# First loads over other queues, identity products ahead of the first tile, and later quarters of the output weights in a two-layer attention kernel

## The chip, the core and the metric

The kernel runs on one core of a Trainium2 chip, in float32 throughout. The metric is the device time of one execution in microseconds (us). A core has a matrix engine (TensorE, PE in the profile, with PEld for its weight loads), VectorE (DVE), ScalarE (ACT), GpSimd (POOL) and SyncE (SP), which only issues transfers. Each works through its own instructions in order. SyncE, ScalarE and GpSimd issue the DMAs, which 16 DMA engines carry out.

## What is computed

The input has 8 images of 32x32 tokens with 512 channels. Layer 0 is a group norm, queries, keys and values by one weight matrix, softmax attention with 8 heads, an output product and a residual. Layer 1 is an attention whose keys and values are sampled at learned positions, then a product with a gelu and a residual.

```
x_norm = group_norm(x, 32 groups) * scale + bias
q, k, v = split(x_norm @ w_qkv + b_qkv)
x = x + softmax(q k^T / 64) v @ w_out + b_out                # layer 0
q = layernorm(x) @ wq + bq;  where = tanh(pw(gelu(depthwise7x7(q))))
kv = bilinear(x, where) @ wv + bv
z = x + softmax((q@mq_w + mq_b) (kv@mk_w + mk_b)^T) (kv@mv_w + mv_b) @ mo_w + mo_b
out = z + gelu(layernorm(z) @ mlp_w + mlp_b)                 # layer 1
```

## The kernel before

**Order of the work.** Layer 0 runs in units: a unit is 128 queries of one pair of heads, so an image has 32 (`per`), and the 8 images have 256. `push` (L206) of a unit emits its scores, then the steps that `run_due` (L371) finds due before the unit's place plus 0.8, then the transposes of the exponentials, every second unit the transfers of both, and then the steps due before the end of the unit. Other work is put into this order by `at(place, step)`, where a place is a number of units. Steps with negative places run ahead of the first unit, sorted by place. The class `InOrder` (L43) fixes each engine's instructions in the order of the program, so all of them carry one line number, L54, in the profile, and one tells them apart by their tiles.

**The start.** Image 0's eight x tiles (128 tokens by 512 channels, 256 KB each) are loaded first (L525 to L530): tiles 0 to 3 by GpSimd's queue, 4 to 7 by SyncE's. SyncE's queue then has three small vectors (gsc, gbi, bqkv, one 4-byte element at a time onto the partitions), then the three 1 MB parts of w_qkv in the order keys (`wB`), queries (`wA`), values (`wC`), and three 256 KB rows (L532 to L537, L550 and L551). `norm_steps` (L569) makes the norm of an image: `turn(t)` transposes tile t by four TensorE products with an identity, and ScalarE copies it out of PSUM into `xT`; `two_tiles` takes statistics of each pair of tiles by four VectorE instructions; `gather`, `means`, `deviations` and `factors` form the group's mean and deviation, with two small TensorE products; `norm` applies them to xT. For image 0 the places are -100 plus `norm_places`, so tiles 0 and 1 are at -91.6 and -91.55, tiles 2 and 3 at -83.6 and -83.55, tiles 4 to 7 at -77.6, -77.55, -76.6 and -76.55. Only then come the keys' products with wB. `turn(0)` and `turn(1)` of image 0 also load the next image's tiles 0 and 1 by GpSimd's queue. PSUM has three buffers for such products, used in turn. `warm(3)`, at two places of the start, gives TensorE three products with an identity (each in two halves, 512 columns) that nobody reads.

**Attention transfers.** The transposed exponentials of two units go through 16 SyncE transfers of 128 KB (`moved`, L222: `et<-sq`), and the products `av<-et,v` of these units follow some three units later (`attention_out`, L767).

**The last image.** Layer 1's weights are folded together while the last image's attention runs (`fold_steps`, L800). The buffer `room_w["w"]`, tag `w`, holds one 1 MB weight matrix at a time; the last image's has wv until its transposes at 23.5 to 24.55 units after the image's begin, then w_out, by quarters of 256 KB that ScalarE's queue issues (`load_quarter`, L545) at 25.2, 25.7, 26.2 and 26.7. Quarters of mv_w follow at 27.2, 27.9, 28.6 and 29.3 by the same queue. The products of the fold that stand among them are at 25.5, 27.5, 28.5, 29.5, 30.5 and 31.5; w_out is first read at 33.1 (`last_places`, L787).

Of the kernel before, what the change touches and what calls it, by code (L numbers as in the profile page):

```python
# [17 lines left out]
P = 128  # L18
# [3 lines left out]
C = 512  # L22
# [4 lines left out]
NQT = QB // P  # L27
NH = 8
HD = 64
# [219 lines left out]
def attention_then_deformable_attention(  # L249
# [30 lines left out]
    nc = tc.nc  # L280
    x_tok = x.rearrange("b h w c -> b (h w) c")
# [8 lines left out]
    ident = const.tile([P, P], F32, tag="ident", name="ident")  # L290
# [7 lines left out]
    def mm_tile():  # L298
        return ps_mm.tile([P, QB], F32, tag="mm", name="mm")

    def by_chunk(w):
        return w.rearrange("(c p) o -> p c o", p=P)
# [65 lines left out]
    def at(place, step):  # L368
        due.append((place, len(due), step))
# [40 lines left out]
    def kept(name):  # L410
        return keep.tile([P, NC, C], F32, tag=name, name=name)
# [98 lines left out]
    with ExitStack() as l0:  # L510
# [3 lines left out]
        nc = InOrder(tc)  # L514
        NX = 2
        NX_T = 3
        xs = {}

        def load_x(b, t):
            if b < B:  # L520
                xs[b, t] = work.tile([P, C], F32, tag="x", name="x", bufs=NX)
                nc.gpsimd.dma_start(xs[b, t], x_tok[b][ts(t, P), :])
# [2 lines left out]
        x2 = work.tile([P, NC, QB], F32, tag="xT", name="x2", bufs=NX_T)  # L525
        for t in range(NQT):
            xs[0, t] = work.tile([P, C], F32, tag="attT", name="x0", bufs=NQB * NHP)
            nc.gpsimd.dma_start(xs[0, t], x_tok[0][ts(t, P), :])
            xs[0, NQT + t] = x2[:, t, :]
            nc.sync.dma_start(xs[0, NQT + t], x_tok[0][ts(NQT + t, P), :])  # L530
        w3 = [kept(name) for name in ("wA", "wB", "wC")]
        gsc = load_cols(wp, gn_scale, "gsc")  # L532
        gbi = load_cols(wp, gn_bias, "gbi")
        bqkv = load_cols(wp, b_qkv, "bqkv")
        for i in (1, 0, 2):
            nc.sync.dma_start(w3[i], by_chunk(w_qkv)[:, :, ts(i, C)])
        bout = load_row(wp, b_out, "bout")  # L537
        room_w = {}

        def load_weight(w):  # L540

            room_w["w"] = work.tile([P, NC, C], F32, tag="w", name="w", bufs=1)
            nc.gpsimd.dma_start(room_w["w"], by_chunk(w))

        def load_quarter(w, c):  # L545
            if c == 0:
                room_w["w"] = work.tile([P, NC, C], F32, tag="w", name="w", bufs=1)
            nc.scalar.dma_start(room_w["w"][:, c, :], by_chunk(w)[:, c, :])
# [10 lines left out]
            out=g3, in_=g3, pattern=[[-GRP, ng], [0, GRP]], compare_op=ALU.is_ge,  # L559
# [3 lines left out]
            out=g3, in_=g3, pattern=[[GRP, ng], [0, GRP]], compare_op=ALU.is_ge,  # L563
# [5 lines left out]
        def norm_steps(b, start, places):  # L569

            room = {}

            def turn(t):
                blk, i = divmod(t, NQT)
                if i == 0:
                    xTs[b, blk] = work.tile([P, NC, QB], F32, tag="xT", name="xT", bufs=NX_T)
                if t == 0:
                    room["stats"] = work.tile([P, NC, NT // 2, 6], F32, tag="stats", name="stats", bufs=1)
                ps = mm_tile()
                for c in range(NC):  # L580
                    nc.tensor.transpose(ps[:, ts(c, P)], xs[b, t][:, ts(c, P)], ident)
                nc.scalar.copy(xTs[b, blk][:, :, ts(i, P)], ps.rearrange("p (c q) -> p c q", q=P))
                if b > 0:
                    load_x(b + (t + NX) // NT, (t + NX) % NT)
                elif t < NX:
                    load_x(1, t)

            def two_tiles(i):
                blk, half = divmod(i, NQT // 2)
                for c in range(NC):  # L590
                    nc.vector.bn_stats(
                        room["stats"][:, c, i, :], xTs[b, blk][:, c, ts(half, 2 * P)]
                    )


            def gather():
                mv = room["mv"] = work.tile([P, NC, 2], F32, tag="mv", name="mv")
                stats = room["stats"]
                for c in range(NC):
                    nc.vector.bn_aggr(mv[:, c, :], stats[:, c, :, :].rearrange("p s f -> p (s f)"))  # L600

            def means():
                mv = room["mv"]
                ps = mm_tile()
                for m in range(2):
                    half = ds(m * HD, HD)
                    nc.tensor.matmul(
                        ps[half, 0:NC], lhsT=gmat[:, half], rhs=mv[:, :, 0], start=True, stop=True
                    )
                mu = room["mu"] = work.tile([P, NC], F32, tag="mu", name="mu")  # L610
                nc.vector.tensor_copy(mu, ps[:, 0:NC])
                dev = room["dev"] = work.tile([P, NC], F32, tag="dev", name="dev")
                nc.vector.tensor_tensor(dev, mv[:, :, 0], mu, ALU.subtract)
                nc.vector.tensor_tensor(dev, dev, dev, ALU.mult)
                nc.vector.tensor_tensor(dev, dev, mv[:, :, 1], ALU.add)

            def deviations():
                ps = mm_tile()
                for m in range(2):
                    half = ds(m * HD, HD)  # L620
                    nc.tensor.matmul(
                        ps[half, 0:NC], lhsT=gmat[:, half], rhs=room["dev"], start=True, stop=True
                    )
                room["rs"] = work.tile([P, NC], F32, tag="rs", name="rs")
                rstd(room["rs"], ps[:, 0:NC], 1e-6)

            def factors():
                nc.vector.tensor_tensor(room["rs"], room["rs"], gsc, ALU.mult)
                room["add"] = work.tile([P, NC], F32, tag="nadd", name="nadd")
                nc.vector.tensor_tensor(room["add"], room["mu"], room["rs"], ALU.mult)  # L630
                nc.vector.tensor_tensor(room["add"], gbi, room["add"], ALU.subtract)

            def norm(blk):
                xT, add, rs = xTs[b, blk], room["add"], room["rs"]
                for c in range(NC):
                    if b == 0 and c % 2 == 0:
                        nc.vector.tensor_scalar(
                            xT[:, c, :], xT[:, c, :], rs[:, c : c + 1], add[:, c : c + 1],
                            ALU.mult, ALU.add,
                        )  # L640
                    else:
                        nc.scalar.activation(
                            xT[:, c, :], xT[:, c, :], AF.Identity,
                            bias=add[:, c : c + 1], scale=rs[:, c : c + 1],
                        )

            steps = [
                *(lambda t=t: turn(t) for t in range(NT)),
                *(lambda i=i: two_tiles(i) for i in range(NT // 2)),
                gather, means, deviations, factors,  # L650
                *(lambda blk=blk: norm(blk) for blk in range(NQB)),
            ]
            for place, what in zip(places, steps):
                at(start + place, what)
# [145 lines left out]
        def fold_steps(first):  # L800
# [41 lines left out]
                nc.scalar.dma_start(raws[name][:, c, :], by_chunk(w)[:, c, :])  # L842

            for c in range(NC):
                at(first + 25.2 + 0.5 * c, lambda c=c: load_quarter(w_out, c))
                at(first + 27.2 + 0.7 * c, lambda c=c: quarter("mv", mv_w, c))
                at(first + per + 1.24 + 0.001 * c, lambda c=c: quarter("wq", wq, c))
            for i, place in enumerate((25.5, 27.5, 28.5, 29.5)):
# [158 lines left out]
        def warm(n):  # L1007
            out = mm_tile()
            for c in range(n):
                for m in range(2):  # L1010
                    half = ds(m * HD, HD)
                    nc.tensor.matmul(
                        out[half], lhsT=ident[:, half], rhs=xTs[0, 0][:, 0, :],
                        start=(c == 0), stop=(c == n - 1),
                    )

        norm_steps(0, -100, norm_places)
        for place in (-76.035, -74.5):
            at(place, lambda: warm(3))
        at(-72.5, lambda: load_weight(w_out))  # L1020
        at(-73, lambda: nc.vector.tensor_scalar(bqkv[:, 0:NC], bqkv[:, 0:NC], 1.0 / HD, None, ALU.mult))

# [13 lines left out]
        for b in range(B):  # L1036
            first = b * per
# [22 lines left out]
            for hp in range(NHP):  # L1060
                for qt in range(NT):
                    n = first + hp * NT + qt
                    if n % per == 0 and b > 0:
# [9 lines left out]
                    t = qkv[b, hp]  # L1073
# [4 lines left out]
                        at=qt % NQT,  # L1078
# [8 lines left out]
    with ExitStack() as l1:  # L1087
        nc = tc.nc


        def pool(name, bufs=1):
            return l1.enter_context(tc.tile_pool(name=name, bufs=bufs, reuse_waits="tile"))

        late, late2, cv, cvhat, first, raw, wp = (
            pool(n) for n in ("late", "late2", "cv", "cvhat", "first", "raw", "w2")
        )
        work = pool("work1", 2)
        nc = InOrder(tc)
# [447 lines left out]
```

## Time and profile before

| what | us |
|---|---|
| median of three runs | 3269.66 |
| lowest, highest | 3261.96, 3269.79 |
| the profiled execution, its own time | 3264.03 |
| its span, from the first to the last instruction | 3262.3 |
| TensorE busy in it | 3217.9 (99%) |
| DVE, ACT, POOL busy | 2522.9, 1780.8, 1593.5 |
| first TensorE product | begins at 8.37 |
| first product of keys | begins at 23.04 |
| longest wait of TensorE after the first 24 us | 2.69, before 2061.11 |

How to read it: the profile is of one execution, with times from its first instruction. "out<-in" are tiles by the program's names, "xN" a number of instructions. "SPq" and "ACTq" are issues of transfers, with the time that the issue held the queue's engine. In the list of waits, "A <- B: total, times, longest" says that A was released by B. PEclk is the granted TensorE clock, 1.00 being full. The trace also records when each of a transfer's 16 parts completed; a transfer has landed with the last.

### The profile page before, as it was taken

How to read it: one execution, taken by the hardware profiler on the slowest of the kernel's cores; microseconds unless marked ns; L12 is line 12 of the kernel's file. 1: busy time of each engine (PE TensorE's matmuls, PEld its weight loads, DVE VectorE, ACT ScalarE, POOL GpSimd, SP SyncE). 2: the span in 40 equal slices, each digit the busy share in tenths (PEclk: the TensorE clock that was granted, in tenths of full speed). 3: DMA queues.
4: the chain of work that ended last, by engine and by line, in shares of the span. 5: the costliest groups of instructions: out<-in, count | busy, mean ns of one | idle time of the engine just before them, and what ended most of it. 6: DMA issues, size and time to landing. Idle time of an engine off the chain costs nothing.

```text
span 3262.3 us, 59564 instructions
## 1 busy us (share of the span) xinstructions
PE 3217.9 (99%) x21588; PEld 1301.2 (40%) x21588; DVE 2522.9 (77%) x3457; ACT 1780.8 (55%) x3826; POOL 1593.5 (49%) x2026
## 2 busy tenths in 40 slices
PE   8999999999999999999999999999999999999999
PEld 4444344344344444444444434333333333333333
DVE  5776778898888888788788888557868787676765
ACT  3443356566567567557657656335555555554442
POOL 1001316755764665664674577225556565653323
PEclk9999999999999999999999999999999999999999
DMA  5666766777677766676676677678777786887873
GB/s 171 169 179 162 210 181 180 211 200 186 204 196 191 203 197 177 204 211 178 181 223 183 177 216 211 180 228 272 219 240 242 228 264 211 264 259 229 265 236 130
DMA packets 479325, 674.31 MB, mean 207 GB/s; under 512 B 76828, under 2 KB 268632, under 8 KB 478776
## 3 DMA queue, kind: packets, MB, share of 16 engines
q1 hardware_dynamic: 434528, 529.53, 56.8%
q0 software_dynamic: 41136, 136.78, 13.7%
q10 hardware_dynamic: 3368, 4.20, 0.4%
q8 instruction: 171, 2.80, 0.4%
q14 instruction: 122, 1.00, 0.1%
HBM read 263.17 MB, written 138.69 MB: 123 GB/s over the span
## 4 chain that ended last, share of the span: by engine, by line
PE 89%; DVE 3%; ACT 2%; DMA 2%; POOL 1%; issue 1%; SPq 1%; POOLq 0%; DVEq 0%; ACTq 0%
PE mm L54 55%; PE sc L54 17%; PE av L54 17%; ACT e L54 1%; DVE nmax L54 1%; SPq L54 1%; DMA et<-sq_d 1%; DVE sq L54 1%; POOL oa L54 0%; DVE chunk L54 0%; DMA w<-in_L_conv_w_out_dram 0%; DMA sq_d<-sq 0%; POOL xr L54 0%; DMA row<-mid,ii 0%; ACT part_x L54 0%
## 5 line engine op out<-in xcount | busy, mean ns | idle before, releaser
L54 ACT ACTIVATE e<-sc,nmax 128x1024 f32<-128x1024 f32 (+1 forms) x1024 | 803.0, 797 | 531.4 <-DVE nmax L54 524.7
L54 DVE TENSOR_REDUCE nmax<-sc 128x1 f32<-128x1024 f32 (+1 forms) x640 | 750.2, 1212 | 291.3 <-PE sc L54 286.0
L54 POOL TENSOR_TENSOR oa<-part_x,oa 128x256 f32<-128x256 f32 x852 | 639.4, 751 | 542.5 <-ACT part_x L54 496.4
L54 DVE STREAM_TRANSPOSE sq<-e 128x1024 f32<-128x1024 f32 x640 | 764.3, 1225 | 118.5 <-ACT e L54 97.7
L54 ACT ACTIVATE part_x<-pad_x,dww_x 128x256 f32<-128x256 f32 x852 | 441.2, 545 | 259.9 <-POOL oa L54 258.4
L54 PE MATMUL sc<-k,q 64*64 64x512 f32 x4096 | 512.3, 603 | 8.8 <-ACT e L54 6.7
L54 PE MATMUL av<-et,v 128*64 128x256 f32 x4096 | 499.2, 386 | 11.7 <-DMA et<-sq 4.5
L54 PEld LDWEIGHTS av<-et,v 128*64 128x64 f32 x4096 | 273.7, 137 | 328.8 <-issue 162.1
L54 POOL TENSOR_TENSOR mv<-mv,minus_half 128x1 f32<-128x1 f32 x128 | 76.3, 596 | 389.0 <-DVE mv L54 388.0
L54 PEld LDWEIGHTS sc<-k,q 64*64 64x64 f32 x4096 | 137.5, 132 | 314.6 <-issue 208.4
L54 POOL TENSOR_TENSOR chunk<-parts,chunk 128x256 f32<-128x256 f32 x240 | 185.3, 772 | 137.2 <-ACT parts L54 123.2
L54 DVE SCALAR_TENSOR_TENSOR od<-pad_x,dww_x,od 128x256 f32<-128x256 f32 x276 | 232.7, 843 | 5.5
L54 PE MATMUL mm<-wo,attH 128*64 128x512 f32 x1024 | 233.7, 598 | 0.0
L54 PE MATMUL mm<-wC,xT 128*64 128x256 f32 x2048 | 232.1, 379 | 0.0
L54 PE MATMUL mm<-xT,wB 128*64 128x512 f32 x1024 | 230.7, 592 | 0.6 <-DVE xT L54 0.6
L54 PE MATMUL mm<-hat_h,wA 128*64 128x512 f32 x1024 | 230.9, 593 | 0.0
L54 PE MATMUL mm<-xT,wA 128*64 128x512 f32 x1024 | 230.7, 592 | 0.0
L54 PE MATMUL mm<-w,attT 128*64 128x512 f32 x1024 | 230.1, 592 | 0.3 <-DMA w<-in_L_conv_w_out_dram 0.3
L54 PE MATMUL mm<-wm,zT 128*64 128x512 f32 x976 | 220.7, 592 | 0.5 <-ACT zT L54 0.5
L54 ACT ACTIVATION_READ_ACCUMULATOR e<-sc,nmax 128x1 f32 x1024 | 209.1, 204 | 0.0
L54 PEld LDWEIGHTS mm<-wC,xT 128*64 128x64 f32 x2048 | 148.0, 137 | 77.7 <-issue 6.4
L54 PE MATMUL mm<-w,hat_x 128*64 128x512 f32 x768 | 170.2, 593 | 0.0
(198 smaller groups left out, 3457.6 us busy)
## 6 DMA issues: line engine op xcount, KB each, us to landing
et<-sq SPq DMA_DIRECT2D x2048, 128.0 KB
sq_d<-sq SPq DMA_DIRECT2D x128, 512.0 KB
et<-sq_d SPq DMA_DIRECT2D x128, 512.0 KB
inv<-rs_d SPq DMA_DIRECT2D x250, 128.0 KB
xr<-mid POOLq DMA_DIRECT2D x64, 256.0 KB
xr<-in_x_dram POOLq DMA_DIRECT2D x62, 256.0 KB
x<-in_x_dram POOLq DMA_DIRECT2D x60, 256.0 KB
out_dram<-res POOLq DMA_DIRECT2D x60, 256.0 KB
```

The source lines that it names most:

```text
L54: return self.tc.keep_in_program_order(op(*args, **kwargs))
```

## The change

Five edits:

1. Image 0's tiles 0 to 3 go by SyncE's queue and 4 to 7 by GpSimd's, the reverse of before.
2. SyncE's queue loads only the queries' and values' weights. The keys' (`wB`) are issued by ScalarE's queue, at place -83.54, which is after ScalarE's copy of tile 3.
3. `warm_ident(5)` is emitted ahead of all steps: five products of the identity with itself, each in two halves of 64 by 128 columns, into a PSUM buffer that nobody reads.
4. The next image's tiles 0 and 1 are loaded at place -70, after the load of w_out, not in `turn(0)` and `turn(1)`.
5. The last image's quarters of w_out are at 29.7, 30.2, 30.7 and 31.2.

```diff
-            nc.gpsimd.dma_start(xs[0, t], x_tok[0][ts(t, P), :])
+            nc.sync.dma_start(xs[0, t], x_tok[0][ts(t, P), :])
             xs[0, NQT + t] = x2[:, t, :]
-            nc.sync.dma_start(xs[0, NQT + t], x_tok[0][ts(NQT + t, P), :])
+            nc.gpsimd.dma_start(xs[0, NQT + t], x_tok[0][ts(NQT + t, P), :])
...
-        for i in (1, 0, 2):
-            nc.sync.dma_start(w3[i], by_chunk(w_qkv)[:, :, ts(i, C)])
+
+        def load_qkv(i, queue):
+            queue.dma_start(w3[i], by_chunk(w_qkv)[:, :, ts(i, C)])
+
+        for i in (0, 2):
+            load_qkv(i, nc.sync)
...
                 if b > 0:
                     load_x(b + (t + NX) // NT, (t + NX) % NT)
-                elif t < NX:
-                    load_x(1, t)
...
-                at(first + 25.2 + 0.5 * c, lambda c=c: load_quarter(w_out, c))
+                at(first + 29.7 + 0.5 * c, lambda c=c: load_quarter(w_out, c))
...
+        def warm_ident(n):
+            out = mm_tile()
+            for c in range(n):
+                for m in range(2):
+                    half = ds(m * HD, HD)
+                    nc.tensor.matmul(
+                        out[half, 0:P], lhsT=ident[:, half], rhs=ident,
+                        start=(c == 0), stop=(c == n - 1),
+                    )
+
         norm_steps(0, -100, norm_places)
+        warm_ident(5)
+        at(-83.54, lambda: load_qkv(1, nc.scalar))
         for place in (-76.035, -74.5):
             at(place, lambda: warm(3))
+        for t in range(NX):
+            at(-70, lambda t=t: load_x(1, t))
         at(-72.5, lambda: load_weight(w_out))
```

## The prediction

> **What bounds the kernel now.** I read first the page's chain of work that ended last: TensorE is 89% of it, and the page has it busy 3217.9 of 3262.3 us. So an edit counts only where TensorE waits or runs slowly, and I looked for these places. Two are near the change. The first is the start, by the chain of the first 24 us (columns: start, length, what; small pieces left out):
>
> ```profile
> 1.39 6.84 DMA x<-in_x_dram
> ...
> 8.37 5.88 PE mm L54 x24
> ...
> 14.27 0.59 ACT xT L54
> ...
> 14.88 2.71 DVE stats L54 x8
> ...
> 19.49 2.93 PE mm L54 x16
> ```
>
> Nothing runs until tile 0 has landed (8.23, by GpSimd's queue); then transposes, copies and statistics follow each other to 17.52. SyncE's and ScalarE's timelines of this stretch (start, length, queue or engine, what):
>
> ```profile
> 0.79 1.81 SPq L54 DMA_DIRECT2D x<-in_x_dram  x4
> 2.65 0.43 SPq L54 DMA_DIRECT2D gsc<-in_L_conv_gn_scale_dram  x1
> ...
> 4.46 7.95 SPq L54 DMA_DIRECT2D wB<-in_L_conv_w_qkv_dram  x1
> 12.45 0.51 SPq L54 DMA_DIRECT2D wA<-in_L_conv_w_qkv_dram  x1
> ```
> ```profile
> 11.71 0.59 ACT L54 COPY xT<-mm 128x512 f32<-128x512 f32 x1 [0.52 <-PE mm L54]
> 12.56 0.59 ACT L54 COPY xT<-mm 128x512 f32<-128x512 f32 x1 [0.27 <-PE mm L54]
> 13.41 0.59 ACT L54 COPY xT<-mm 128x512 f32<-128x512 f32 x1 [0.27 <-PE mm L54]
> 14.27 1.64 ACT L54 COPY xT<-mm 128x512 f32<-128x512 f32 x3 [0.27 <-PE mm L54]
> ```
>
> The issue of wB held SyncE for 7.95 us. The copies stand 0.85 us apart up to 14.27 and closer after it: four transposes take 0.85 us with 230 ns weight loads up to 14.2, and 0.43 us with 140 ns ones from 14.4. So TensorE ran at half its later rate for 6 us, though PEclk shows 1.00 there.
>
> The second place is the last image's stretch by TensorE's timeline, SyncE's list of waits, and the table by windows (length, engines' busy time, PEclk, DMA share, GB/s):
>
> ```profile
> 2061.11 2.51 PE L54 MATMUL av<-et,v 128*64 128x256 f32 x16 [2.69 <-DVE rs L54]
> 2063.34 4.84 PE L54 MATMUL mm<-raw 128*64 128x512 f32 x16
> ```
> ```profile
> SPq L54 <- DMA raw<-in_L_conv_mv_w_dram: 5.5, 2, 4.6
> ...
> SPq L54 <- DMA w<-in_L_conv_w_out_dram: 4.8, 2, 4.4
> ```
> ```profile
> 2061.10:2066.00 4.90, 4.89 (x24) 2.74 (x26) 2.46 (x3) 1.03 (x2) 3.08 (x4) 0.65 0.74 181
> ```
>
> The wait of 2.69 is named after VectorE, but the last of the 16 transfers of et landed at 2060.92; it was that. SyncE stood from 2043.1 to 2047.55 before the third of them. SyncE's and ScalarE's transfers take eight completion counters in turn, and an issue waits until the counter's transfer before it has landed. The counter here was the second quarter of w_out's, issued by ScalarE at 2042.22 and landed at 2047.53. So 4.4 us of SyncE's wait became TensorE's 2.69, and the clock, granted at 0.65 in the last row, took more: 2.51 and 4.84 us where the same groups take 1.95 and 3.60 elsewhere, 1.8 us.
>
> **The change, part by part.**
>
> *Tiles swapped.* The landings belong to the queues: SyncE's tiles landed at 3.50, 4.11, 9.24 and 9.85 (the last two by one or two late engines of 16), GpSimd's at 8.23, 9.40, 10.51 and 11.20. Swapped, tiles 0 and 1 are transposed at about 4 to 6.5, and then TensorE waits for tile 2 until 9.24. Tile 2 began at 10.55 before, so 1.25 us are won there. From 9.3 on, six tiles at the slow 0.85 us end at 14.4; no later tile waits (11.20 is the latest landing). Tile 7's copy ends at 14.4 + 0.2 + 0.6 = 15.2 (before: 15.91), its four statistics of 0.33 at 16.6 (before: 17.52): **-0.9**. `warm(3)` (2.79) then runs at the fast rate from 14.45 to 17.25, just in time for the next product. If tiles 2 and 3 land with their first 14 engines (6.6 and 7.8) and the transposes run at the fast rate, GpSimd's last tile at 11.20 sets the end: 11.65 transposed, 12.4 copied, and VectorE's 2.7 us of the last two pairs done by about 14.6: -2.9.
>
> *Identity products.* Five, two halves each: between 5 x 0.21 and 5 x 0.43 us by the transposes' and the three-product group's rows, from about 2.6 (identity written at 2.51). They end by 4.8, a little after tile 0's landing at 3.50, and the wait for tile 2 hides that: 0. I give them no gain either, since TensorE is idle again from 6.5 to 9.3 before the bulk of the transposes. Without that wait they would cost tile 0 up to 1.3 us. The trace needed six busy us, transposes alone, before the rate rose. The Trainium skill, "TensorE: Matmul & The Clock Gate", Part 4, says that transposes do not count as activity for the clock; here the rate doubled in the midst of transposes, so I go by the row. By the page the identity products would be the only activity before `warm`, and all transposes would stay slow: that sum is also -0.9.
>
> *wB on ScalarE.* Copies 4 to 7 and the norm are queued behind this issue, and TensorE's tile 7 waits for copy 4's buffer. It costs from 0.34 (ScalarE's own quarters of w_out) to 7.95 (wB on SyncE). I take 0.5, as wA and wC took, since that queue is empty. It begins after copy 3, at 11.85; copy 4 would have begun at 12.05, so 0.3 is late there and is caught up by copy 6: 0. Should it take gsc's counter, it waits for 12.72 at most, which costs about 0.3. SyncE's long issue becomes wA's. wA and wB then move together: wB, wA and wC landed 2.7 us apart (17.34, 20.05, 22.76), so the two take 5.4 from about 13.3 and are there by 19. Keys' products can begin at 22.1, so it is covered by 3 us; without that cover each late us counts. The skill's "DMA: Bandwidth & Descriptors", section "Issuing engines are not separate DMA queues", speaks against this edit: another issuer saves issue time alone. The trace's 392 GB/s with one queue agrees, and nothing is claimed for it here.
>
> *Next image's tiles.* Two issues of 0.55 us leave GpSimd's queue at 5.2 and come back at 21.9, ahead of bq_x, dww_x and a memset of 1.4 us that are used units later; the tiles are first read some 60 us after. 0. Their 0.5 MB leave the stretch up to 12.5, which helps gsc.
>
> *Quarters of w_out later.* Counters go round in the program's planned order, not by when ScalarE really issues. Without the quarters the 16 transfers begun at 2041.84 take 16 x 0.652 and 2.7 to land, 2055 against the need at 2058.4. The stall goes, and the slow clock with it: -2.69 - 1.8 = **-4.5**. What is late next: the quarters now stand around the transfers that begin at 2075.11. In the order of before, a quarter at a place ending in .2 fell behind 10 or 11 of the sixteen two units earlier, at .7 behind 12, 16 or 6. Carried over, the last mv quarter holds the first of these transfers by 0.9 us, w_out's quarters the third by 1.1 and the seventh by 1.7: 3.7 together, against a slack of 2.3 (landed at 2087.6, used at 2090.06). A new stall of 3.7 - 2.3 = **+1.4**; from 0 (planned otherwise) to 4.5 (the whole of the old one). I take 1.4, without a slow clock, since gaps of about 1 us (1.06 at 356.9, 0.98 at 421.9) had none. w_out lands near 2086, some 10 us before it is read at 2100.43.
>
> **Sum.** -0.9 - 4.5 + 1.4 = -4.0. From the profiled execution, 3264.03 (span 3262.3 and 1.7 around it), that is 3260.0. That execution lies 5.6 under the median of the runs, 3269.66. The four shown (3261.96, 3264.03, 3269.66, 3269.79) spread over 7.8 us, and nothing tells which level the next will have, so I set the sum against their mean, 3266.4: **3262.4**.
>
> **The rivals.**
> - *The stall only moves* (chance 0.25). The later quarters meet the last sixteen transfers with the old 2.69 and the slow clock. For it: the mechanism is the same and the slack is 2.3. Against: DMA engines are busier in the old place (share 1.00 at 2047 to 2053, 0.72 at 2072 to 2078). Only -0.9 is left: 3265.5.
> - *Both parts in full* (0.2): tiles 2 and 3 not late, no new stall: -2.9 - 4.5 = -7.4, 3259.0. Against: the late engines are there in the trace.
> - *ScalarE held by wB* (0.1). The issue lasts 7.95 us there too, from 11.85 to 19.8, if what held SyncE is not SyncE's queue alone. Copies 4 to 7 then run to 22.1 and statistics to 23.4, 5.9 later than before; with -3.1 of the last image the kernel is slower by 2.8: 3269.2. Statistics end 3.6 us after copy 4 begins, so the start loses from an issue that ends after 13.9, and the whole from 17.0. Against: wA, behind wB on the same queue, took 0.51.
> - *The start does not move* (0.05): the products or the wait of the counter take what the swap gives; -3.1, 3263.3.
>
> The forecast has 0.4. **Range:** the best case from the lowest run is 3254.6, the held ScalarE from the highest 3272.6; with 2 in 10 left outside, 3256 to 3271. About 0.3% (9.8 us) is what a measurement of this kernel can tell from no change. No case alone reaches it; but with runs that spread over 7.8, a median under 3259.9 comes about in half of the full case and a sixth of the others but the held one: 0.1 + 0.12 = 0.22 faster. Slower needs 3279.5, the held case from the highest level and more: 0.03. Within 0.3%: 0.75.
>
> **What would show it.** Right: TensorE's first transposes of x near 4, a wait of some 3 us for tile 2, copy 7 done near 15.2, keys' products from about 22.1; no wait before `av` near 2057, PEclk 1.00 there, SyncE's waits for w_out's quarters 30 us later and a wait of TensorE of 1 to 2 us near 2085. Wrong: an issue of wB on ACTq of several us, tiles 2 and 3 landing elsewhere than near 9.5, the rate of the transposes doubling before tile 4, or the old wait still there.

## The result, and the profile after

The changed kernel is slower by 0.3%: median 3274.27 us (22 runs, 3267.66 to 3293.23) against 3265.27 for the kernel before (22 runs, 3257.91 to 3272.07), ratio 1.0029 with a 95% interval of [1.0020, 1.0038]. The forecast was 3262.4, which is 4.0 below the 3266.4 that it was set against; the result is 9.0 above the kernel before. The profiled execution after took 3270.45 us, its span is 3268.6; before, 3264.03 and 3262.3.

I set the two traces side by side by the begin of each unit's first exponential (ScalarE's `e<-sc`), which both have in the same order. After minus before, in us:

| at unit | difference | what lies between this row and the one above |
|---|---|---|
| 0 | -2.15 | the start |
| 58 (469 us) | -3.2 | |
| 83 (679 us) | +0.55 | a wait of 2.71 before `av` at 614.58, and a half clock from 614.5 to 617.9 |
| 242 | +1.8 | small waits |
| 253 | -2.7 | the old wait at 2061 is gone |
| 256 | +4.5 | a wait of 3.16 at 2090.23, and one of 4.08 at 2164.56 with a half clock |
| end of the span | +6.25 | |

The start, by the changed kernel's TensorE timeline (start, length, what, count, and in brackets the wait ahead of it):

```profile
2.57 2.40 PE L54 MATMUL mm<-ident 128*64 128x128 f32 x20 [2.57 <-POOL ident masks.py:199]
4.90 1.97 PE L54 MATMUL mm<-ident,x 128*128 128x128 f32 x8
7.42 0.63 PE L54 MATMUL mm<-ident,x 128*128 128x128 f32 x4 [0.56 <-DMA x<-in_x_dram]
8.65 2.46 PE L54 MATMUL mm<-ident,x 128*128 128x128 f32 x20 [0.60 <-DMA x<-in_x_dram]
...
15.95 4.25 PE L54 MATMUL mm<-xT,ident 128*64 128x512 f32 x12
20.89 1.51 PE L54 MATMUL mm<-xT,wB 128*64 128x512 f32 x6 [0.69 <-DVE xT L54]
```

The identity products end at 4.97 and hold tile 0, which landed at 3.52. Tiles 2 and 3 are waited for by 0.56 and 0.60 us, not by 3, since they landed at 7.29 and 8.51. From 8.65 on, 20 transposes take 2.46 us; before, 24 took 5.88. The keys' products begin at 20.89 (23.04 before). But the second `warm(3)` takes 4.25 where the first took 2.79. The table by windows shows why (length, busy time of the engines with counts, PEclk, DMA share, GB/s); the second row is the long wait behind the last image:

```profile
17.10:20.60 3.50, 3.10 (x8) 0.60 (x4) 0.85 (x4) 2.45 (x4) 3.50 (x7) 0.51 1.06 389
2164.00:2168.00 4.00, 3.44 (x18) 1.95 (x20) 0.50 (x1) 0.48 (x1) 0.00 (x0) 0.57 0.98 390
```

SyncE's and ScalarE's timelines show the issues: wA, now first of the big ones on SyncE, held it 4.41 us, and wB on ScalarE took 0.45, between the copies (the first block is SyncE's, the second ScalarE's).

```profile
4.82 4.41 SPq L54 DMA_DIRECT2D wA<-in_L_conv_w_qkv_dram  x1
9.27 0.75 SPq L54 DMA_DIRECT2D wC<-in_L_conv_w_qkv_dram  x1
```
```profile
9.31 0.59 ACT L54 COPY xT<-mm 128x512 f32<-128x512 f32 x1 [0.64 <-PE mm L54]
9.32 0.45 ACTq L54 DMA_DIRECT2D wB<-in_L_conv_w_qkv_dram  x1
9.81 2.05 ACT L54 COPY xT<-mm 128x512 f32<-128x512 f32 x4
```

The last image: no wait is left at 2061, and TensorE's timeline has two others. SyncE's list of waits (2036 to 2130) shows the quarters still there, with shorter stalls than before.

```profile
2090.23 1.95 PE L54 MATMUL av<-et,v 128*64 128x256 f32 x16 [3.16 <-DMA et<-sq]
2164.56 8.44 PE L54 MATMUL mm<-smp,wC 128*64 128x256 f32 x60 [4.08 <-DVE smp L54]
```
```profile
SPq L54 <- DMA raw<-in_L_conv_mv_w_dram: 4.0, 3, 2.4
SPq L54 <- DMA w<-in_L_conv_w_out_dram: 2.2, 2, 2.0
```

The wait of 4.08 stands where the kernel before had 1.08 (next line), in a part of layer 1 (its sampled keys) that no line of the diff touches:

```profile
2161.47 7.02 PE L54 MATMUL mm<-smp,wC 128*64 128x256 f32 x60 [1.08 <-DVE smp L54]
```

GpSimd's timeline shows what came late: the second gather of rows, `row<-mid,ii`. In the changed kernel:

```profile
2140.66 1.53 POOL L54 DMA_INDIRECT row<-mid,ii  x1 [0.34 <-issue]
2149.38 0.98 POOL L54 DMA_INDIRECT row<-mid,ii  x1 [7.18 <-DVE smp L54]
```

and in the kernel before:

```profile
2140.58 1.53 POOL L54 DMA_INDIRECT row<-mid,ii  x1 [0.34 <-issue]
2142.41 1.50 POOL L54 DMA_INDIRECT row<-mid,ii  x1 [0.30 <-DVE hat L54]
```

Edit 4 explains it. It takes the first request for a buffer of tag `x` from `turn(0)` to place -70, and in the compiled programs the addresses follow the order of first requests. The tiles `mv`, `mu`, `col`, `dev`, `rs` and `nadd` moved down by some 4 KB, from 105344 and up to 101248 and up, and the x tiles from 101248 to 109760, behind them. The buffer of that second gather (99456 to 101504 in a partition) now overlaps the place of `col`, the fold's bias columns, which has the tag of layer 0's `mu`. The gather's instruction carries other waits: for the transfers `col<-row_b` and for the addition on VectorE that reads the second of them. Both come late, at 2148.59 and 2148.77 (ScalarE's and VectorE's timelines of the changed kernel):

```profile
2146.48 0.38 ACTq L54 DMA_DIRECT2D col<-row_b  x1
2148.61 0.16 DVE L54 TENSOR_TENSOR bqq<-col,bqq 128x4 f32<-128x4 f32 x1 [1.57 <-DMA col<-row_b]
```

The view names `smp` as releaser, since it was VectorE's last instruction before the gather; the semaphore's count in the program is that of the addition.

### The profile page after: what moved, and what is told of

It is laid out like the page before. It is cut to its first block, busy times and chain, and to the rows that moved or that the text cites. A ratio compares the mean times of both kernels' runs of the same rounds, so it can differ in the third digit from the quotient of the medians.

```text
span 3268.6 us, 59601 instructions
## 1 busy us (share of the span) xinstructions
PE 3222.2 (99%) x21608; PEld 1308.5 (40%) x21608; DVE 2524.4 (77%) x3457; ACT 1780.8 (54%) x3826; POOL 1594.0 (49%) x2026
## 4 chain that ended last, share of the span: by engine, by line
PE 89%; DMA 3%; DVE 2%; ACT 2%; POOL 2%; SPq 1%; issue 1%; POOLq 0%; ACTq 0%; DVEq 0%
PE mm L54 55%; PE sc L54 17%; PE av L54 17%; SPq L54 1%; ACT e L54 1%; DMA et<-sq 1%; DVE sq L54 1%; DMA et<-sq_d 1%; DMA sq_d<-sq 1%; DVE nmax L54 1%; POOL oa L54 0%; DMA rs_d<-rsT 0%; POOL xr L54 0%; DMA inv<-rs_d 0%; ACT part_x L54 0%
```

## Experiments

All are measured beside runs of the kernel before on the same chip. Ratios are to it, with 95% intervals. Theories go by letters in the expectations: A, the addresses cost the time; B, the later quarters do; C, the earlier start is given back later.

**Next image's tiles alone** (edit 4 on the kernel before):

```diff
-                elif t < NX:
-                    load_x(1, t)
...
+        for t in range(NX):
+            at(-70, lambda t=t: load_x(1, t))
```

> The kernel before with edit 4 alone (the next image's two tiles loaded at place -70). Theory A (place in memory): the tile tag x gets its place later, so in layer 1 the second gathered row lies on layer 0's col tiles; the second gather waits some 5 us more for their loads, TensorE waits about 4 us before mm<-smp,wC (1.1 before) and its clock then drops: slower by 3 to 5 us. Theory B (the quarters of w_out do it): no change, and 1.1 us before mm<-smp,wC.

3270.18 against 3265.26, 1.0018 [1.0009, 1.0027]. TensorE's wait is there, and the 60 records behind it take 8.61 us (7.02 before): a half clock follows.

```profile
2165.21 8.61 PE L54 MATMUL mm<-smp,wC 128*64 128x256 f32 x60 [5.11 <-DVE smp L54]
```

The same later load **with the tiles requested where they were** tells the addresses from the load itself (the request stays in `turn`, the load goes to place -70):

```diff
-                    load_x(1, t)
+                    xs[1, t] = work.tile([P, C], F32, tag="x", name="x", bufs=NX)
...
+        for t in range(NX):
+            at(-70, lambda t=t: nc.gpsimd.dma_start(xs[1, t], x_tok[1][ts(t, P), :]))
```

> The kernel before with the next image's first two tiles loaded at place -70, and the tiles allocated where they were, so that every address stays. Theory A (the whole cost of that edit is the addresses): within 1 us of the kernel before, about 3265.3, and the wait of TensorE before the means of layer 1 (mm <- smp,wC, near 2164) is 1.0 to 1.4 us, not 4 to 5. Rival D (the later load itself takes what the start gains, since 0.5 MB then meet other transfers): 3267 to 3270.

3263.37 against 3264.03, 0.9997 [0.9986, 1.0008]; the wait is 0.71 and the second gather follows the first at once, as before:

```profile
2162.78 7.03 PE L54 MATMUL mm<-smp,wC 128*64 128x256 f32 x60 [0.71 <-DVE smp L54]
2142.24 1.54 POOL L54 DMA_INDIRECT row<-mid,ii  x1 [0.33 <-issue]
2144.08 1.50 POOL L54 DMA_INDIRECT row<-mid,ii  x1 [0.31 <-DVE hat L54]
```

So theory A holds: the load's place costs nothing that can be told (-0.7), and the addresses cost 4.9 us. In the trace of the tiles alone that is the wait, 5.11 for 1.08, and the half clock behind it, 8.61 for 7.02. The second gather is late in the two traces with the addresses moved, and in no other.

**Quarters alone** (edit 5: `25.2` becomes `29.7`):

> The kernel before with edit 5 alone (quarters of w_out 4.5 units later). Theory A: TensorE's wait of 2.7 near 2061 goes and one of about 3 comes near 2094, 1.1 us before mm<-smp,wC as before: within 2 us of the kernel before. Theory B: the later quarters cost the 9 us: slower by 5 us or more, with the wait of 4 us before mm<-smp,wC.

3263.21 against 3265.26, 0.9993 [0.9981, 1.0006]. Theory B falls: this edit isn't the loss. Nor is it the gain of 4.5. The old wait is gone, and TensorE's timeline has the new one:

```profile
2097.78 3.54 PE L54 MATMUL av<-et,v 128*64 128x256 f32 x16 [2.54 <-DMA et<-sq]
```

2.54 of waiting, and 3.54 for a group that takes 1.95 at full clock: 4.1 given back of 4.5. This execution has two more waits before `av`, 4.30 at 1142.74 and 3.71 at 1672.27, which are not the edit's; they are taken up below.

**The start's edits and the whole, with the addresses kept** (edits 1 to 4, then 1 to 5, with x tiles requested as above):

> Edits 1 to 4 without 5, with the next image's tiles given their place in memory where they had it before and only loaded later. Theory A: keys' products begin 2 to 3.6 us earlier, everything else as before: faster by 2 to 4 us. Theory C (the start shifts the transfers against each other and costs time later): same or slower, with a new wait of 2 us or more between 100 and 2000 us, as the one at 614 in the changed kernel's profile.

3270.21, 1.0010 [0.9996, 1.0025]. The new wait between 100 and 2000 us that theory C asked for isn't in its trace; but this profiled execution took 3263.72, 6.5 less than the median, so the trace need not show what the median lost.

> The changed kernel, the next image's tiles given their place in memory as before. Theory A: 1.1 us before mm<-smp,wC, the wait of 3 near 2090 stays: 4 to 5 us faster than the changed kernel, so 0 to 4 slower than before by the measured +9, or 1 to 3 faster by the traces. Theory B: as slow as the changed kernel, +9.

3268.61, 1.0015 [1.0004, 1.0027]: 5.7 under the changed kernel, as theory A says, but still above the kernel before, though in the trace the first unit begins 1.8 sooner. Something behind the start seems to take more than that back. So each edit of the start was tried alone.

**Swap alone** (edit 1: `gpsimd` and `sync` exchanged in the two lines), twice:

> The kernel before with the first image's first four tiles on SyncE's queue and the next four on GpSimd's, nothing else. Theory E (the start's gain is real and lasts; what was lost behind it in the runs with the start edits came from something else): first transposes near 4.9, keys' products near 22, 0.5 to 2 us under the kernel before, 3263.3 to 3264.8. Rival F (the swap moves later work so that waits appear): 3267 to 3270, with a wait of TensorE of over 1.5 us that the kernel before does not show.

3265.93 against 3264.03, 1.0011 [1.0001, 1.0020].

> The tiles swapped alone, once more, to settle a question of size: its one profiled execution was 4.2 us under that of the kernel before, its median 1.9 above. Theory E (the start's gain lasts): median 1 to 3 us under the kernel before. Rival F (a start that is earlier loses the gain again between 60 and 2050 us, in waits before av <- et that fall at random): median 0 to 3 us over it.

3263.86 against 3267.73, 0.9991 [0.9982, 1.0001]. The two disagree; the first alone would have been read as a loss. With 11 or 12 runs, 2 us are not told apart by one comparison, and I go by several from here on. In both traces the first unit is earlier than in that of the kernel before, by 3.4 and 1.4.

**wB on ScalarE alone** (edit 2):

```diff
-        for i in (1, 0, 2):
-            nc.sync.dma_start(w3[i], by_chunk(w_qkv)[:, :, ts(i, C)])
...
+        for i in (0, 2):
+            load_qkv(i, nc.sync)
...
+        at(-83.54, lambda: load_qkv(1, nc.scalar))
```

> The kernel before with the keys' weights issued by ScalarE at place -83.54, after the column loads' wait, nothing else. Theory E: keys' products within 0.5 us of the kernel before's (23.04), total 3264.8 to 3266. Rival G (ScalarE's issue is the one that costs, by holding ScalarE's copies or by bringing the weights late): keys' products 1 to 4 us later, total 3267 to 3270.

3265.93 against 3264.03, 1.0010 [1.0001, 1.0019]. The issue is short, but the keys' products wait for the weights:

```profile
23.68 3.65 PE L54 MATMUL mm<-xT,wB 128*64 128x512 f32 x16 [1.92 <-DMA wB<-in_L_conv_w_qkv_dram]
```

**Identity products alone** (edit 3: `warm_ident(5)` ahead of the first step):

> The kernel before with the twenty identity products ahead of the first transposes, nothing else. By the prediction: no effect, 3265.3, since TensorE stands idle again before the first tile. What the changed kernel's trace suggests (its clock was full at 6.93, amid the transposes): the clock rises up to 2 us sooner than in the kernel before, 3263.5 to 3265. Rival H (the products' buffer or their time holds up the first transposes): keys' products later than 23.04, 3266 or more.

3265.28 against 3264.03, 1.0011 [0.9998, 1.0024]. The first unit is 1.1 earlier than in the trace before, but no earlier than in that of the quarters alone, whose start is the old one.

**Swap and quarters**, with every address as before, and the same with **the 1 MB load of w_out cut into pieces**, the pieces also alone. The suspect was this load, at place 9.95 of an image, behind which the transfers of `et` take up to 11 us to land; the waits before 614, 1142 and 1672 end 19 to 21 us after it. In the diff, `load_piece` issues a quarter of the load by GpSimd's queue.

```diff
-                    for place, w in ((0.95, w_out), (7.6, wq), (9.95, w_out), (15.6, wq)):
+                    for place, w in ((0.95, w_out), (7.6, wq), (15.6, wq)):
...
+                    for c, place in enumerate((9.95, 9.96, 10.7, 10.95)):
+                        at(first + place, lambda c=c: load_piece(w_out, c))
```

> The tiles swapped and the last image's quarters 4.5 units later, nothing else: the two edits that took time out of their own stretch, with every address as in the kernel before. Theory E: 3 to 5 us under the kernel before (2 to 3 of the start, 1 to 2 of the quarters). Rival F: 0 to 2 us from it, with a wait of 2 us or more before av <- et near 614, 877, 1140 or 1670 in the profile.

3263.39 against 3267.73, 0.9993 [0.9983, 1.0003].

> The kernel before with the 1 MB load of w_out that GpSimd issues once in each image from the third on, at place 9.95, cut into four loads of 256 KB at places 9.95, 9.96, 10.7 and 10.95. Rival F's cause (the scores' transposes queue behind that load, so that TensorE waits 2 to 4 us at some image in some executions): spread of the runs smaller, median 1 to 3 us under the kernel before. If that load has no part in it: within 1 us of the kernel before, or above it if a piece comes late for the projection.

3285.16, 1.0059 [1.0043, 1.0075].

> Swap, quarters and pieces together. If the load is what takes the start's gain back: 4 to 7 us under the kernel before, and under the swap with the quarters. If not: as the swap with the quarters, within 1 us.

3282.12, 1.0052 [1.0035, 1.0068]. The pieces failed for another reason, so they say nothing on the suspect: the last one, issued at 1142.53, comes late for the projection, in every image from the third on.

```profile
1144.11 1.08 PE L54 MATMUL mm<-w,attT 128*64 128x512 f32 x4 [0.37 <-DMA w<-in_L_conv_w_out_dram]
1146.64 1.79 PE L54 MATMUL mm<-w,attT 128*64 128x512 f32 x4 [1.45 <-DMA w<-in_L_conv_w_out_dram]
```

**The whole, addresses kept, without one of the start's edits**; and two kernels once more:

> The changed kernel with the addresses kept and the identity products left out. Theory I (what still costs with the addresses kept are the identity products: the clock is full some 6 us sooner, at 5.5 to 7, but a stretch of half clock of 3.4 us follows before 20 in all three executions with them and the swap, and in none of the other starts): no half clock before 200 us, median 2 to 5 us under the kernel with everything and the addresses kept. Rival K (the keys' weights on ScalarE cost it): as that kernel, within 1 us. Rival R (nothing does: that kernel's 3.3 us above the kernel before are chance): all four within 2 us of one another and of the kernel before.

3262.40 against 3264.87, **0.9989 [0.9981, 0.9998]**: under the kernel before by 2.5 us, in one comparison, whose interval just leaves out 1, and under the changed kernel's 3274.27.

> The changed kernel with the addresses kept and the keys' weights issued by SyncE, ahead of the queries', as before. Theory I: half clock again before 20 us, median as that of the kernel with everything and the addresses kept, within 1 us. Rival K: 2 to 5 us under it. Rival R: all four within 2 us of one another.

3267.10, 1.0013 [1.0004, 1.0021].

> The whole change with the addresses kept, once more. Theories I and K: 2 to 5 us over the kernel before. Rival R: within 2 us of it.

3265.69, 1.0007 [0.9996, 1.0018].

> Swap and quarters alone, once more, to settle whether this part of the change beats the kernel before. Theories I, K and R alike: 2 to 4 us under the kernel before, as its one measurement had it; the quarters' 4.5 us given back at one wait near 2086, the start's 2 kept. If the first measurement was chance: within 1 us.

3261.82, 0.9998 [0.9989, 1.0007].

So in the whole change the identity products cost: here the kernel with them (h3) is 3.3 above the one without (h1), and theory K falls, since without wB on ScalarE (h2) the time is no lower than with it. Alone (f4) they cost nothing that can be told: +1.3, where the other single edits beside it were at -0.7, +1.9 and +1.9. Of the mechanism that theory I gave, half falls: a half clock before 20 us is in neither of these last two traces with them (the traces' records of the full clock begin at 12.14 and 8.08, and the next half clock is at 1930 and 2087), and the time is lost all the same. So two other ways were tried: the products take one of PSUM's three buffers and so shift all later ones, and they put ten instructions ahead of all of TensorE's code.

```diff
-        warm_ident(5)
+        for n in (2, 2, 1):
+            warm_ident(n)
```

> The whole change with the addresses kept, its ten identity products spread over three buffers of PSUM, so that every later product uses the buffer that it uses in the kernel before (one buffer more, of three, had shifted them all). Theory L (the shifted buffers are what costs 3 to 5 us behind the start): 2 to 4 us under the kernel before, as without the products. Theory I (the products at the start, by the clock) and theory M (ten more instructions ahead of all of TensorE's code): 1 to 4 us over the kernel before, as with all the products in one buffer.

3269.02 against 3266.11, 1.0013 [1.0000, 1.0025]. Theory L falls.

```diff
-        warm_ident(5)
...
-        for place in (-76.035, -74.5):
-            at(place, lambda: warm(3))
+        at(-76.035, lambda: warm_more(5))
+        at(-74.5, lambda: warm(3))
```

Here `warm_more(5)` is `warm(3)` and then the ten identity products into the same buffer.

> The whole change with the addresses kept, its ten identity products moved behind the first three warming products at place -76.035, into their buffer: the same ten instructions, no buffer more, and no work before the first tile. They take some 1.2 us at full clock, in TensorE's waiting time or beside it. Theory I and theory L: 1 to 3 us under the kernel before (the start without them, less at most 1.2). Theory M: 1 to 4 us over the kernel before.

3269.64 against 3266.11, 1.0013 [1.0001, 1.0025]. Theory I falls as well: moved behind the transposes, the products can't act on the first tiles, and the loss is the same. What theory M says of the time holds: in the whole change the loss is there with the ten instructions, wherever they stood. Median minus median of before, over all kernels with the addresses kept and w_out in one piece:

| identity products | kernels | differences, us | mean |
|---|---|---|---|
| present | e3, e4, f4, h2, h3, i1, i2 | +4.9, +3.4, +1.3, +2.2, +0.8, +2.9, +3.5 | +2.7 |
| absent | e2, f1, f2, f3, g1, g2, h1, h4 | -2.1, -0.7, +1.9, +1.9, -3.9, -4.3, -2.5, -3.1 | -1.6 |

The two groups differ in other edits too; the match is h1 against e4, h3, i1 and i2.

How ten instructions do it stays open. The traces give hints and no proof. Queue q8, of kind "instruction", brings 171 packets of 16 KB, one each 19 us or so. The page before counts 21588 products of TensorE and as many weight loads, some 252 records for each packet, so I take these packets for TensorE's code; no run shows that directly. With the ten instructions they lie elsewhere in the program. One of them begins at 109.2 to 111.4 us in all eight traces with the products, and at 115.0 to 119.7 in all ten without (w_out in one piece). The DMA views by windows of the last kernel, 106 to 114, and of h1, 114 to 122, show one packet each (queue, kind: packets, MB, share):

```profile
q8 instruction: 1, 0.02, 1.1%
```
```profile
q8 instruction: 1, 0.02, 0.7%
```

Waits of 2 us or more before `av` between 100 and 1950 us are in 4 of the 8 traces with the products (the changed kernel's 614.58, e4's 1141.74, h2's 1929.73 and the last kernel's 1142.51) and in 1 of the 10 without (e2's two); two more of these ten have one just past that stretch (2.53 before 1998.25 in the kernel before, 2.23 before 1997.40 in e1). Another place differs as well. TensorE's wait before `mm<-smp,wC`, with the addresses kept, is 0.71 to 1.33 in the nine traces without the products. With them it is 0.44 to 1.32 in four and 2.17, 2.19 and 3.52 in three (h3, e3, i2), though the second gather follows the first at once in these. That is the right direction, and too few to show it. Moving the ten instructions behind the first image's units, where only the later code would shift, wasn't tried.

## Why the prediction was wrong, step by step

- **Next image's tiles, costed 0: the step that failed.** I had asked who reads the tiles and who is queued behind the loads, and that part was right (f1: -0.7). I didn't ask what the moved request does to the addresses of everything requested after it. It measured +4.9 alone; in the traces that is one wait with the half clock behind it, 2100 us later, in another layer.
- **Identity products, costed 0: the second step that failed.** My reason against a gain was that TensorE stands idle again before the bulk of the transposes. It stood 0.56 and 0.60 us, and the trace's record of the full clock begins at 6.93 (14.36 before), so in this execution the transposes ran fast earlier, in part given back by a half clock at 17.2. With the products alone (f4) TensorE did stand, 2.48 us for tile 0, and the record begins at 12.17. What I missed is behind it: the kernel with everything, addresses kept, is at +3.4 and +0.8, without the products at -2.5 (measured once), so they cost some 4.6 there. How is open. A cost that is not at the place of the edit had no term in my sum. On the Trainium skill's rule ("TensorE: Matmul & The Clock Gate", Part 4) that transposes do not count as clock activity: before, the clock record begins at 14.36, and in the second trace with the swap alone at 13.92, both times ahead of the first product that isn't a transpose (15.16 and 14.03). So the row decides, as it did in the prediction.
- **Quarters later, -4.5 and +1.4.** The first term was right for the profiled execution: the difference falls by 4.5 between units 242 and 253. But its 1.8 of slow clock was that execution's. Eight traces have the quarters in the old place and w_out in one piece (before, e1, e3, f1, f2, f3, f4, g1); all have the old wait, of 1.71 to 3.33, and a half clock follows it in two of them, before and f1. The second term was mis-sized. I took 1.4, without a slow clock, from a slack and a guess of the order; the wait measured 3.16 in the changed kernel, and 2.54 and 2.94 in e2 and h1, there with a half clock. Over the ten traces with the later quarters it is 2.40 to 3.44, and a half clock follows in eight. So the edit takes away a wait that mostly costs itself alone and brings one that mostly costs the clock too; why the clock falls more often there isn't shown. The holds of SyncE came near in sum (with the units' shift of 2.69 taken off, 1.8 for the first transfer, 0.1 for the third, 2.0 for the seventh, where I had 0.9, 1.1 and 1.7), but the last of the sixteen then took 3.7 to land, and 2.7 before. Alone the edit is worth 2.1 by medians, inside its interval. This is the rival "the stall only moves", to which I gave 0.25, with the mechanism that I had named: the same counters, next to the next sixteen transfers.
- **Tiles swapped, -0.9.** The way was right, the size wrong. The wait of 3 us for tile 2 on which the sum was built is there in some executions (3.30 in g1, 2.73 in h4, 2.78 in h1) and not in others (0.56 in the changed kernel, 0.70 in f2, 1.46 in g2). With it the first unit came 1.4 and 1.8 earlier (g1, h4), without it 3.4 and 3.1 (f2, g2), where I had 0.9 and, as the best case, 2.9. But the old start varies as well: the keys' products begin at 21.87 to 23.64 in five traces with the old first loads (before, e1, e2, f1, g3; mean 22.7), and at 19.62 to 21.61 in five with the swap as the only edit of the start (f2, g1, g2, h4, g4; mean 20.7). So the swap is worth some 2.0 at the start, not 0.9. In the changed kernel they came 2.15 earlier than in the profiled kernel before.
- **wB on ScalarE, 0.5 and nothing net.** The issue was right (0.45). The cover of 3 us was not: wB landed at 19.2 as I had said, but the start had become faster, so 1.7 were left, and in two other executions (f3 and h3) TensorE waited 1.92 and 1.84 for it. The rival "ScalarE held by wB" fell: no copy came late.

The sum as measured: the change without the identity products and with the addresses kept -2.5, the products +4.6, the addresses +4.9, together +7.0 against +9.0 found. The rest is within what such medians leave open: the addresses' interval alone goes from 2.9 to 8.8. The sum of -4.0 was a sum of places that the diff touches; the two terms that decided, +4.6 and +4.9, were at none of them. No rival of mine had them either.

## What to carry to other kernels

When a line that requests a buffer is moved, compare the addresses and the waits of all later instructions, not only who reads that buffer; where a load is to move and its buffer need not, keep the request where it was. A stall taken away from transfers that share counters with others is worth what it cost only if the new place was checked for the same meeting. And in a kernel whose runs spread over 14 us (3257.91 to 3272.07 before), a profile shows where time goes in one execution, but an edit worth 2 us needs several comparisons of medians: one of 11 runs gave 1.0011 for a swap, the next 0.9991.

## What the runs showed of the hardware

Ten small products by TensorE, 1.26 to 2.40 us of work that nobody reads, cost the whole change about 4 us, at each of the places of the start where they stood; alone they cost nothing that could be told, and how they cost is open. In the 20 traces TensorE has 26 waits of 2.5 to 5.1 us between 100 and 2200 us; at 18 of them the clock is at half for 3.4 us, in two for 6.8; 3.4 us of it add up to 1.7 (2165.21: wait 5.11, then 8.61 for what took 7.02). And the start varies by 2 us between executions with the same order of loads: TensorE's wait for tile 2 was 0.70 in f2 and 3.30 in g1, which is the same kernel.
